# Attention kernel with a learned gate: how one right-hand operand of the gate product is formed in the setup

## The chip, the cores and the metric

The kernel runs on one core of a Trainium2 chip. The metric is device time in microseconds (us), the median of several executions. Lower is better. The core has five engines that run beside each other, each with its own queue of instructions worked off in order: TensorE (PE) multiplies matrices, VectorE (DVE), ScalarE (ACT) and GpSimd (POOL) work element by element, and SyncE (SP) issues DMAs. GpSimd issues DMAs as well, among them those that add what they bring to what is there.

## The reference

```python
memory_proj = einsum('bme,de->bmd', memory, W_mem)
scores = einsum('bnd,bmd->bnm', x, memory_proj) / sqrt(D)
attn = softmax(scores)
memory_context = einsum('bnm,bmd->bnd', attn, memory_proj)
gate = sigmoid(einsum('bnf,df->bnd', concat([x, memory_context]), W_gate) + b_gate)
fused = x + gate * memory_context
out = fused * rsqrt(mean(square(fused)) + EPS) * norm_w
```

Everything is float32. `x` is 8 x 1024 x 1024, the memory 8 x 64 x 512, `W_mem` 1024 x 512, `W_gate` 1024 x 2048.

## The kernel before

**The product with W1.** The gate needs `x` times the half of `W_gate` that meets `x`, here W1, 1024 x 1024. It is made for 512 rows of `x` at a time, 16 times (`q` = 0 to 15), by a scheme of Strassen's kind on two levels. The outer level cuts 512 x 1024 and W1 into quarters and needs seven *outer products* instead of eight, in the order 1, 6, 7, 5, 4, 2, 3 (`ORDER`). Each is split once more into seven *inner products* of TensorE, with the names `af`, `kB`, `kC`, `ed`, `ed`, `af`, `af` after the PSUM tiles that take them. The inner products need sums of quarters on both sides.

**Left sums** are made anew for every `q`. The outer ones (`s1` to `s4`, and one in place of the block `a21`) are made by VectorE (`outer_s`), from blocks of `x` that VectorE has transposed (`transpose_x`, L377). The inner ones (`l2`, four of 128x256 for each outer product) are made by GpSimd (`inner_s`). The `l2` tiles have two buffers. In the profile buffer numbers are left out, so `l2`, `t4` and `it4` are `l`, `t` and `it` there.

**Right sums** depend on W1 alone. They are made once, in the setup, and stay for all 16 blocks of rows. W1's quarters lie in two tiles `w1_0` and `w1_1`; `outer_b[2]`, the one this case is about, is the first half of `w1_1`. The outer operands 5, 7, 6 and 4 are formed from them one after another, where `W(h, c)` is a quarter in device memory:

- `t5` = quarter 7 - quarter 1, a VectorE subtraction of 128x2048 (`outer_sum`)
- quarter 7 in place: its negative by ScalarE (`outer_negative`, L216), then an adding DMA from GpSimd's queue brings `W(1, 1)` (`outer_add`, L220)
- `t6`: the negative of `t5`, then an adding DMA of `W(1, 1)`
- `t4`: the negative of `t6`, then an adding DMA of `W(1, 0)`

For every outer operand `inner_sum` makes four inner sums of 128x512: T1, T2, the quarter R12 in place, and T4. T1, T2 and T4 go to a tile `it`. `w1_place(o)` allocates the tiles. The sum of R12 overwrites a block of `t6`, so `t4`'s reading of `t6` has to come first.

**What sets the order.** The order is written by hand. All of these instructions are issued in program order on their engine (`pin`). The setup is a straight piece of code that ends with the memory side: `mg`, the projected memory times the other half of `W_gate`, is stored to `mgd` and read back by `load_mg`. The main loop counts slots, one for each inner product. `at(slot, ...)` puts an instruction behind a slot, and `mid` beside the work of an outer product. In the first 512 rows some right sums are still made in slots: those of operand 4 on GpSimd in slot 4, those of 2 and 3 on VectorE.

**What the rest of the first rows needs from those engines.** GpSimd adds parts of the products to the gate (`pre`, tile `gate`) and issues the DMA that adds the bias to `mg` (`add_bias`, L542). VectorE makes the sums `u` that free the PSUM banks of `kB` and `kC`, and adds `ed` and `af` to the gate. Before outer product 4 is over, `visit` adds the attention part on TensorE (tile `pc`), in the banks of its `kB` and `kC`.

Of the kernel before, what the change touches and what calls it, by code (L numbers as in the profile page):

```python
# [20 lines left out]
def tile_gated_cross_attention_rmsnorm(  # L21
# [42 lines left out]
    nc = tc.nc  # L64
# [30 lines left out]
    def tt(eng, o, a, b, op):  # L95
        pin(eng.tensor_tensor(o, a, b, op))  # L96
# [7 lines left out]
    def rows_by_chunk(w, n):  # L104

        return w.rearrange("(p j) f -> p j f", j=n)
# [57 lines left out]
    def w1_place(o):  # L164

        if o in (5, 6, 4):
            outer_b[o] = const.tile([P, 4, H], F32, tag=f"t{o}", name=f"t{o}")
        inner_t[o] = const.tile([P, 3, 2, C], F32, tag=f"it{o}", name=f"it{o}")

    def w_op(o, s):  # L170
        if s >= T4:
            return inner_t[o][:, s - T4, :, :]
        k, n = {R11: (0, 0), R21: (1, 0), R12: (0, 1), R22: (1, 1)}[s]
        return outer_b[o][:, 2 * k : 2 * k + 2, n * C : (n + 1) * C]
# [37 lines left out]
    def outer_sum(o, a, b):  # L212
        tt(nc.vector, outer_b[o], outer_b[a], outer_b[b], ALU.subtract)

    def outer_negative(o, b):
        pin(nc.scalar.activation(outer_b[o], outer_b[b], AF.Copy, scale=-1.0))  # L216

    def outer_add(o, h, c):
        rows = rows_by_chunk(w_gate_t[:D, :], KD)[:, 4 * h : 4 * h + 4, c * H : (c + 1) * H]
        pin(nc.gpsimd.dma_start(outer_b[o], rows, accum_op=ALU.add))  # L220

    def inner_sum(eng, o, n):
        s, a, b = ((T1, R12, R11), (T2, R22, T1), (R12, R22, R12), (T4, R21, T2))[n]
        tt(eng, w_op(o, s), w_op(o, a), w_op(o, b), ALU.subtract)
# [369 lines left out]
    def mg_product(l, r, pgs, start=False):  # L594
        for t in range(2):
            for k in range(KH):
                mm(pgs[t], l[:, k, t * P : (t + 1) * P], r[k], start and k == 0, k == KH - 1)
# [132 lines left out]
    for o, a, b in ((T1, w_op(7, R12), p11), (T2, p22, w_op(7, T1)), (R12, p22, w_op(7, R12)), (T4, p21, w_op(7, T2))):  # L730
        tt(nc.vector, w_op(7, o), a, b, ALU.subtract)
    w1_place(4)
    outer_negative(4, 6)
    for n in range(4):
        inner_sum(nc.gpsimd, 6, n)
    outer_add(4, 1, 0)
    mg_product(m22, b11, both)
    mg_copy(c21, both)
    store_mg(c21, 1, 0)
# [14 lines left out]
    def at(slot, fn, *args):  # L754
        due.setdefault(slot, []).append(lambda: fn(*args))
# [56 lines left out]

    for o in (2, 3):
        w1_place(o)
    for n in range(4):
        at(4, inner_sum, nc.gpsimd, 4, n)
    for s, o, n in ((3, 2, 0), (4, 2, 1), (5, 2, 2), (6, 2, 3), (11, 3, 0), (14, 3, 1), (14, 3, 3)):
        at(s, inner_sum, nc.vector, o, n)
# [416 lines left out]
```

## Time and profile before

| | us |
|---|---|
| median of 3 runs (950.52 to 951.43) | 951.36 |
| the profiled execution | 951.43 |
| its span, first to last instruction | 949.4 |
| busy in the span: DVE | 795.9 |
| busy in the span: ACT | 442.8 |
| busy in the span: POOL | 731.8 |

A row of a timeline reads: start, duration, engine, line, operation, `output<-inputs`, shape, count, and in brackets how long the engine stood idle before it and what ended that. Rows of one kind that follow each other are merged, so a duration can hold several instructions, and the durations of matmuls overlap a little. Nearly all helpers record their instructions in one line (`L93` for matmuls, `L96` for sums of two tensors), so the names of the tiles tell more than the line. In a table of stages each engine has its busy time and, in brackets, its count of instructions, in the order PE, PEld (weight load), DVE, ACT, POOL; the clock that TensorE was granted, the DMA share and GB/s follow.

### The profile page before, as it was taken

The page shows a single profiled execution, that of the slowest core. Times are in us where ns is not written, and L with a number is a line of the kernel's source. Part 1 is how long each engine was busy: PE and PEld are TensorE (multiplying, and loading weights), DVE is VectorE, ACT ScalarE, POOL GpSimd, SP SyncE. Part 2 cuts the span into 40 slices and gives each one's busy share as a digit, 9 for nine tenths or more (in the row PEclk, how much of TensorE's full clock was granted, in tenths as well). Part 3 has the DMA queues.
Part 4 walks back from the last instruction along what each step waited for, and adds up shares of the span by engine and source line. Part 5 has one row for each costly group of instructions (what it writes and reads, how often), then busy time and mean ns, then how long its engine had stood idle before and what let it go on. Part 6 is the DMA issues. An engine that isn't in the chain of part 4 may idle for free.

```text
span 949.4 us, 15989 instructions
## 1 busy us (share of the span) xinstructions
PE 934.1 (98%) x5584; PEld 733.4 (77%) x5584; DVE 795.9 (84%) x1275; ACT 442.8 (47%) x1125; POOL 731.8 (77%) x818
## 2 busy tenths in 40 slices
PE   9999899999999999999999999999999999999995
PEld 8746678787777878787777878787777878787774
DVE  6886688888898889888898889888897889888887
ACT  4343227364553627264553617264553617264556
POOL 4994978868696868868696868868696868868695
PEclk9999899999999999999999999999999999999998
DMA  9978197391927557391927456391927457391642
GB/s 376 309 157 189 23 155 156 75 204 45 203 87 151 117 124 154 78 201 45 208 81 156 111 127 151 79 204 41 209 81 156 112 126 153 81 205 40 133 154 89
DMA packets 72768, 131.59 MB, mean 139 GB/s; under 512 B 12656, under 2 KB 49520, under 8 KB 72432
## 3 DMA queue, kind: packets, MB, share of 16 engines
q1 hardware_dynamic: 61920, 93.86, 37.6%
q0 software_dynamic: 10768, 36.70, 21.3%
q8 instruction: 45, 0.74, 0.3%
q14 instruction: 35, 0.29, 0.1%
HBM read 90.70 MB, written 41.68 MB: 139 GB/s over the span
## 4 chain that ended last, share of the span: by engine, by line
PE 86%; POOL 6%; DVE 3%; DMA 3%; issue 1%; ACT 0%; POOLq 0%; DVEq 0%; ACTq 0%
PE af L93 30%; PE ed L93 20%; PE pc L93 10%; PE kC L93 10%; PE kB L93 10%; PE psT_af L93 5%; DMA t<-in_w_gate_t 3%; POOL it L96 1%; POOL gate L96 1%; POOL mg_right L96 1%; DVE gate L96 1%; POOL t_w L96 1%; POOL w L96 1%; POOL l L96 1%; DVE pm_it L96 0%
## 5 line engine op out<-in xcount | busy, mean ns | idle before, releaser
L96 POOL TENSOR_TENSOR gate<-gate,u 128x512 f32<-128x512 f32 (+1 forms) x224 | 244.9, 1107 | 152.1 <-DVE u L96 151.1
L833 ACT ACTIVATE gate<-gate 128x512 f32<-128x512 f32 x127 | 79.9, 630 | 183.4 <-DVE gate L96 182.1
L377 DVE STREAM_TRANSPOSE a<-xq 128x512 f32<-128x512 f32 x128 | 141.3, 1108 | 8.4 <-PE af L93 8.0
L96 POOL TENSOR_TENSOR l<-a 128x256 f32<-128x256 f32 x128 | 109.9, 859 | 15.9 <-PE af L93 15.9
L93 PE MATMUL kB<-it,l 128*128 128x256 f32 x448 | 116.1, 382 | 4.4 <-POOL l L96 4.4
L93 PE MATMUL pc<-mg,attnT 64*64 64x512 f32 x512 | 117.1, 596 | 0.1
L93 PE MATMUL ed<-it,l 128*128 128x256 f32 x448 | 115.1, 380 | 0.0
L862 DVE SCALAR_TENSOR_TENSOR gate<-gate,ss,nw_sb 128x512 f32<-128x512 f32 x120 | 110.4, 920 | 1.1
L1087 ACT COPY u<-af 128x256 f32<-128x256 f32 x112 | 41.4, 370 | 128.8 <-PE af L93 112.6
L93 PE MATMUL af<-w,a 128*128 128x256 f32 x384 | 98.6, 379 | 0.0
L93 PEld LDWEIGHTS kB<-it,l 128*128 128x128 f32 x448 | 85.7, 192 | 16.2 <-POOL l L96 4.8
L96 DVE TENSOR_TENSOR gate<-gate,ed 128x512 f32<-128x512 f32 x112 | 76.4, 682 | 25.0 <-POOL gate L96 23.1
L96 DVE TENSOR_TENSOR gate<-gate,pc 128x512 f32<-128x512 f32 x128 | 85.5, 677 | 11.8 <-ACT gate L833 11.8
L93 PEld LDWEIGHTS ed<-it,l 128*128 128x128 f32 x448 | 85.5, 191 | 11.4
L96 DVE TENSOR_TENSOR gate<-gate,af 128x512 f32<-128x512 f32 (+1 forms) x128 | 76.0, 604 | 13.3 <-PE af L93 10.5
L96 POOL TENSOR_TENSOR l<-s 128x256 f32<-128x256 f32 x96 | 83.5, 869 | 2.5 <-ACT u L1087 2.5
L93 PEld LDWEIGHTS af<-w,a 128*128 128x128 f32 x384 | 73.1, 190 | 10.2 <-issue 0.5
L93 PEld LDWEIGHTS pc<-mg,attnT 64*64 64x64 f32 x512 | 32.8, 132 | 49.7 <-issue 23.2
L93 PE MATMUL ed<-it,a 128*128 128x256 f32 x256 | 68.2, 390 | 0.0
L93 PE MATMUL af<-mg,attnT 64*64 64x512 f32 (+1 forms) x380 | 67.1, 457 | 0.0
L93 PE MATMUL kC<-w,l 128*128 128x256 f32 x256 | 66.6, 384 | 0.0
L96 DVE TENSOR_TENSOR u<-u,kB 128x256 f32<-128x256 f32 x112 | 45.8, 409 | 24.5 <-PE kB L93 23.7
(234 smaller groups left out, 2140.3 us busy)
## 6 DMA issues: line engine op xcount, KB each, us to landing
xq<-in_x SPq DMA_DIRECT2D x64, 512.0 KB, 10.4
gate<-in_x POOLq DMA_DIRECT2D x60, 512.0 KB, 8.5
out<-gate SPq DMA_DIRECT2D x60, 512.0 KB, 2.9
w<-in_w_gate_t SPq DMA_DIRECT2D x8, 512.0 KB, 10.2
w<-in_w_gate_t SPq DMA_DIRECT2D x2, 2048.0 KB, 16.9
mg<-mgd SPq DMA_DIRECT2D x16, 256.0 KB, 4.7
wm<-in_w_mem_t SPq DMA_DIRECT2D x4, 512.0 KB, 6.0
mpd<-mpT SPq DMA_DIRECT2D x4, 512.0 KB, 9.5
```

What stands on the lines that cost most here:

```text
L93: pin(nc.tensor.matmul(o, lhsT, rhs, start=start, stop=stop, skip_group_check=True))
L96: pin(eng.tensor_tensor(o, a, b, op))
L377: nc.vector.transpose(A[key][:, :, r * P : (r + 1) * P], chunks(xq[q][:, 4 * t : 4 * t + 4, :], KD)[:, half * KH : (half + 1) * KH],)
L833: pin(nc.scalar.activation(g, g, AF.Sigmoid))
L862: nc.vector.scalar_tensor_tensor(g[:, cols], g[:, cols], rstd[:, t % 2 : t % 2 + 1], nw_sb[:, cols], ALU.mult, ALU.mult,)
L1087: pin(nc.scalar.copy(p1, af[:, 0]))
```

## The change

`t4` is formed in one step on VectorE, quarter 2 less `t6`, where the negative on ScalarE and the adding DMA stood. Two of its four inner sums, T1 and T2, move from slot 4 of the main loop to the place in the setup where the adding DMA was issued. The other two stay in slot 4.

```diff
     w1_place(4)
-    outer_negative(4, 6)
+    outer_sum(4, 2, 6)
     for n in range(4):
         inner_sum(nc.gpsimd, 6, n)
-    outer_add(4, 1, 0)
+    for n in range(2):
+        inner_sum(nc.gpsimd, 4, n)
     mg_product(m22, b11, both)
...
-    for n in range(4):
+    for n in (2, 3):
         at(4, inner_sum, nc.gpsimd, 4, n)
```

On VectorE, at the end of the sums for operand 7 in the setup, the rows before were these (`it7` and `w1_0` belong to operand 7, `a22` is a transposed block of `x`, `s1` and `s2` are outer left sums, `u0` is a sum that frees a PSUM bank):

```order
L96 TENSOR_TENSOR w1_0_113<-pm_ed1_143,w1_0_113 128x2x256
L96 TENSOR_TENSOR it7_437<-w7_b_438,it7_437 128x512
L377 STREAM_TRANSPOSE a22_0_482<-xq0_306 128x4x128 x2
L96 TENSOR_TENSOR s1_0_490<-a21_0_429,a22_0_482 128x1024
L96 TENSOR_TENSOR s2_0_503<-s1_0_490,a11_0_426 128x1024
L96 TENSOR_TENSOR u0_1_512<-u0_1_512,kB0_1_519 128x256
```

Now, at the same place:

```order
L96 TENSOR_TENSOR w1_0_113<-pm_ed1_143,w1_0_113 128x2x256
L96 TENSOR_TENSOR it7_437<-w7_b_438,it7_437 128x512
L96 TENSOR_TENSOR t4_463<-w1_1_114,t6_399 128x2048
L377 STREAM_TRANSPOSE a22_0_483<-xq0_306 128x4x128 x2
L96 TENSOR_TENSOR s1_0_491<-a21_0_429,a22_0_483 128x1024
L96 TENSOR_TENSOR s2_0_504<-s1_0_491,a11_0_426 128x1024
L96 TENSOR_TENSOR u0_1_513<-u0_1_513,kB0_1_520 128x256
```

The sum for `t4` stands ahead of the last transposes of the first rows, so ahead of `s1` and `s2`, which need them. It reads `t6` and so waits for the adding DMA of `t6`.

On GpSimd, from the last sums of operand 6 to the left sums of outer product 7 (`l2_0_6` and `l2_0_7` are left sums of the products 6 and 7), the difference is:

```order
 L96 TENSOR_TENSOR t6_399<-t6_399 128x2x256
 L96 TENSOR_TENSOR it6_400<-t6_399,it6_400 128x512
-L220 DMA t4_463<-in_w_gate_t 128x4x512
-L96 TENSOR_TENSOR l2_0_6_516<-s2_0_503 128x256
-L96 TENSOR_TENSOR l2_0_6_516<-l2_0_6_516,s2_0_503 128x256
-L96 TENSOR_TENSOR l2_0_6_516<-s2_0_503 128x256
-L96 TENSOR_TENSOR l2_0_6_516<-s2_0_503,l2_0_6_516 128x256
 L96 TENSOR_TENSOR it4_464<-t4_463 128x512
 L96 TENSOR_TENSOR it4_464<-t4_463,it4_464 128x512
+L96 TENSOR_TENSOR l2_0_6_517<-s2_0_504 128x256
+L96 TENSOR_TENSOR l2_0_6_517<-l2_0_6_517,s2_0_504 128x256
+L96 TENSOR_TENSOR l2_0_6_517<-s2_0_504 128x256
```

The DMA is gone, and two of the `it4` sums stand ahead of the left sums of product 6 instead of behind them. The other two, and the left sums of product 7, follow as before. On ScalarE only the negative of `t6` is gone.

## The prediction

> **What bounds the kernel now.** I read the page's head first, then who TensorE (PE) waits for, then PE's timeline round the wait, and last the timelines of the three engines that feed it.
>
> ```profile
> span 949.4 us, 15989 instructions
> ...
> PE 934.1 (98%) x5584; PEld 733.4 (77%) x5584; DVE 795.9 (84%) x1275; ACT 442.8 (47%) x1125; POOL 731.8 (77%) x818
> ...
> PE kB L93 <- POOL l L96: 4.4, 1, 4.4
> PE pz L93 <- DVE zeros L116: 1.2, 1, 1.2
> ```
>
> PE is the bound: busy 98% of the span. Setup work matters only where PE waits for it, and in the view of PE's waits only two are listed. One is the start. The other is a single wait of 4.4 us, of a `kB` product for an `l` sum of GpSimd (POOL).
>
> ```profile
> 87.74 1.13 PE L93 MATMUL af<-t,s 128*128 128x256 f32 x4
> ...
> 93.89 1.03 PE L93 MATMUL af<-w,a 128*128 128x256 f32 x4
> 99.28 2.08 PE L93 MATMUL kB<-it,l 128*128 128x256 f32 x4 [4.36 <-POOL l L96]
> 101.14 1.92 PE L93 MATMUL kC<-w,l 128*128 128x256 f32 x4
> 102.85 1.79 PE L93 MATMUL ed<-it,a 128*128 128x256 f32 x4
> ...
> 107.07 1.03 PE L93 MATMUL af<-t,s 128*128 128x256 f32 x4
> ...
> 123.10 1.03 PE L93 MATMUL af<-w,a 128*128 128x256 f32 x4
> ...
> 129.15 1.03 PE L93 MATMUL af<-w,s 128*128 128x256 f32 x4
> ```
>
> PE's timeline shows the place. Outer product 7 of the first 512 rows begins at 93.89, outer product 5 at 107.07: 13.18 us. Undisturbed, seven inner products take 129.15 - 123.10 = 6.05 us, 0.86 each. So **product 7 loses 13.18 - 6.05 = 7.13 us**: 4.36 of waiting, and 2.77 more because the rows behind the wait are 1.8 to 2.1 us long instead of 1.03. The stages say why; the column behind POOL is the granted PE clock:
>
> ```profile
> 98.00:100.00 2.00, 0.72 (x2) 0.64 (x3) 0.00 (x0) 0.00 (x0) 1.92 (x4) 0.50 0.00 0
> 102.00:104.00 2.00, 2.00 (x6) 1.65 (x5) 1.97 (x4) 0.37 (x1) 1.92 (x3) 0.50 0.00 0
> 106.00:108.00 2.00, 2.00 (x11) 1.77 (x10) 1.90 (x4) 1.63 (x8) 1.52 (x2) 1.00 0.00 0
> ```
>
> The clock is 0.50 behind the wait and 1.00 again by 106. Why GpSimd was late is in its own timeline:
>
> ```profile
> 69.79 1.29 POOL L96 TENSOR_TENSOR it<-t 128x512 f32<-128x512 f32 x1 [1.28 <-DMA t<-in_w_gate_t]
> ...
> 73.62 2.25 POOL L96 TENSOR_TENSOR it<-t,it 128x512 f32<-128x512 f32 x1
> 75.82 1.29 POOL L220 DMA_DIRECT2D t<-in_w_gate_t  x1
> ...
> 81.72 1.17 POOL L96 TENSOR_TENSOR l<-s,l 128x256 f32<-128x256 f32 x1
> 92.70 1.27 POOL L96 TENSOR_TENSOR it<-t 128x512 f32<-128x512 f32 x1 [9.80 <-DMA t<-in_w_gate_t]
> ...
> 97.70 0.72 POOL L96 TENSOR_TENSOR l<-a 128x256 f32<-128x256 f32 x1
> 98.50 0.72 POOL L96 TENSOR_TENSOR l<-l,a 128x256 f32<-128x256 f32 x1
> ...
> 100.54 1.94 POOL L96 TENSOR_TENSOR gate<-gate,u 128x512 f32<-128x512 f32 x2
> ...
> 129.00 1.27 POOL L96 TENSOR_TENSOR gate<-gate,u 128x512 f32<-128x512 f32 x1 [1.48 <-DVE u L96]
> ```
>
> The adding DMA for `t4` is issued at 75.82, and GpSimd then stands 9.80 us for its landing, with the four sums of `it4` and the four of `l` for product 7 queued behind. PE's `kB` needs the second `l` sum, which ends at 99.22; it starts at 99.28.
>
> **The change part by part.** *Removed: the wait for the DMA.* `t4` becomes a VectorE (DVE) sum, so GpSimd never stands for a landing at 92.70. What is late next is either one of GpSimd's own earlier jobs or an input of `l`. I follow both, against these DVE rows:
>
> ```profile
> 70.23 0.68 DVE L96 TENSOR_TENSOR it<-w_b,it 128x512 f32<-128x512 f32 x1
> 71.32 2.13 DVE L377 STREAM_TRANSPOSE a<-xq 128x512 f32<-128x512 f32 x2 [0.41 <-PE pm_ctx L93]
> 73.49 1.26 DVE L96 TENSOR_TENSOR s<-a,a 128x1024 f32<-128x1024 f32 x1
> 78.19 1.23 DVE L96 TENSOR_TENSOR s<-s,a 128x1024 f32<-128x1024 f32 x1 [3.44 <-PE pm_ed L93]
> ...
> 88.59 1.22 DVE L96 TENSOR_TENSOR a<-a,a 128x1024 f32<-128x1024 f32 x1
> ...
> 101.84 0.69 DVE L96 TENSOR_TENSOR gate<-gate,ed 128x512 f32<-128x512 f32 x1 [9.06 <-POOL gate L96]
> ```
>
> *Added: one DVE sum of 128x2048, behind the row at 70.23.* The setup has one of the same shape (`t5`), beside two GpSimd subtractions:
>
> ```profile
> 27.15 3.14 DVE L96 TENSOR_TENSOR t<-w 128x2048 f32<-128x2048 f32 x1 [0.58 <-DMA w<-in_w_gate_t]
> ...
> 26.88 1.28 POOL mg_right L96
> 28.22 3.20 POOL mg_right L96
> ```
>
> DVE's 3.14 us include waiting: GpSimd's first subtraction ends at 28.16, DVE at 30.29, so the sum itself is about 2.13, and GpSimd's second takes 3.20 instead of 1.28. The two take turns. Bounds 2.13 to 3.14. I take 2.13 from the end of GpSimd's running subtraction (69.79 + 1.29 = 71.08), so `t4` is ready at **73.2** (at most 74.1).
>
> *What is queued behind it on DVE:* two transposes (2.13), the sum `s1` (1.26) and `s2` (1.23). They end at 75.3 and about 76.9. The sum `s2` can't begin before 78.15, when PE lets its buffer go: 3.44 us of idle time hide the added sum, at worst with a port turn of about 1.3 too many.
>
> *SyncE's (SP's) queue:* the next `x` load waits for the transposes, so it goes 2 to 3 us later (75.3 to 76.5). Its first transpose stands beyond 108 now; the landing takes at most 17.8 us in the view of that tile (estimate: by 94.3). Hidden. The stores and the load of `mg` behind it are the third rival.
>
> *GpSimd:* the second sum of `it6` waits out the DVE sum (to 74.5), and its third waits for it by dependence: DVE reads the block that this sum overwrites. They end at 75.7 and, with a DVE turn of 1.1, at 78.1. Then the two new `it4` sums, 2 x 1.27 and a turn of 1.2 for `s2`: 81.8. Now the `l` sums of product 6, first at 79.56 before, begin 2.3 us later. Four take 2.9 (97.70 to 100.54), so the second ends at 83.3, at most 84.5 with a small DVE turn each. PE's `kB` of product 6 starts at 87.74 + 0.97 = 88.71. Hidden, with 4 us in hand. The last two `it4` sums then end between 87.2 and 89.4.
>
> *Moved: the `l` sums of product 7.* Their operand is the `a<-a,a` sum of DVE, ready at 88.59 + 1.22 = 89.8 (91.1 if a GpSimd sum of 1.27 gets ahead of it). So GpSimd is there in time, or nearly, and DVE's sum sets the start. The second `l` ends 1.52 us later (97.70 to 99.22), at **91.3 to 92.6**. PE wants it at 93.89 + 2 x 0.43 = 94.75. The wait goes, with 2.1 to 3.4 us in hand, and with it the slow clock: 7.13 us on PE.
>
> *Removed as well:* ScalarE's (ACT's) negative (1.9 us) and GpSimd's issue (1.29). Neither was on a path that PE felt; I count nothing.
>
> *What is late next.* From 92.70 on GpSimd has no idle time of a microsecond until 129.00, and DVE stands 9.06 us for its `gate` sum. They run just ahead of PE:
>
> ```profile
> 115.49 0.40 DVE L96 TENSOR_TENSOR u<-u,kB 128x256 f32<-128x256 f32 x1
> ...
> 115.94 0.65 PE L93 MATMUL pc<-mg,attnT 64*64 64x512 f32 x2
> ```
>
> Ten inner products after 107.07 PE could start `pc` at 107.07 + 6.05 + 3 x 0.86 = 115.70; it starts at 115.94, behind DVE's `u` at 115.89. So `pc` sits at the meeting of two chains. PE's moves by 7.13, or 7.37 if those 0.24 go too. The GpSimd and DVE chain moves by as much as the `gate` sum of 100.54: it now begins when the four `l` sums end, 2.9 us after 89.8 to 91.1, and up to 0.6 later for the one DVE sum that falls among them: 92.7 to 94.6, or **7.8 to 5.9 us earlier**. Most of that span lies beyond or at PE's 7.13. I take 7.0.
>
> Sum: 951.43 (the profiled execution: span 949.4 and 2.0 around it) - 7.0 = **944.4 us**. It is 0.07 above the median of 951.36, which changes nothing.
>
> Two rules of the Trainium skill, weighed. SBUF — State Buffer (Who interferes with whom) says that VectorE and GpSimd share one port pair under an exclusive lock, held for a whole instruction. That speaks against a 2.13 us sum put into GpSimd's busiest stretch. The row of 3.20 agrees. With every turn charged by that rule (2.13 and 1.07 twice, 0.55 four times), GpSimd comes to the `l` sums at an estimated 89.4, and without it at 84: both before 89.8, so the sum is the same.
>
> TensorE: Matmul & The Clock Gate (What's actually happening) says that an idle window of about 3.4 us halves the clock, and a busy one restores it. At half rate for one such window the loss here would be 4.36 + 1.7 = 6.1 us, an estimate, and the time 945.4. The rows show 2.77 for the slow part, and I use these.
>
> **The rivals.**
>
> *1. The feeding chain decides.* If port turns fall badly, `gate` begins at 94.6 or a little later, and `pc` waits up to 2 us for DVE. Gain 5 to 6.5: 945 to 946.5 us. For it: DVE and GpSimd are both full there, and `pc` follows DVE within 0.05 us already. Against: `l` waits for one early DVE sum, not for GpSimd.
>
> *2. The wait moves to `t6` and the kernel gets slower.* DVE now stands in order for the adding DMA of `t6`, which only ACT and GpSimd did.
>
> ```profile
> 69.80 1.92 ACT L216 ACTIVATE t<-t 128x2048 f32<-128x2048 f32 x1 [7.46 <-DMA t<-in_w_gate_t]
> ...
> DMA to landing us min/median/max: 8.9/11.4/16.8
> ```
>
> Issued at 58.27, it landed at 69.7, 1.2 us before DVE gets there. If it lands d later, GpSimd comes to the `l` sums of product 7 not at 87.2 to 89.4 but d later. From d = 3.8 to 6.0 on (arrival after 94.75 - 1.52 = 93.2) `kB` waits again, and from d = 8.3 to 10.5 on (arrival after 97.70, as now) the kernel is slower than before, by each further us. With a landing at 82 (d = 12.3) that is 1.8 to 4.0 us: 953.2 to 955.4. For it: the same kind of DMA took 16.8 when the `x` load ran beside it (d = 5.4: `gate` begins 2.2 to 5.0 earlier than now, 946.4 to 949.2 us). Against: what runs before 69.7 is unchanged, and the `x` load is still issued behind it.
>
> *3. The gain is handed to `mg`.* GpSimd's bias DMA waits for the second `mg` load, which waits for a store.
>
> ```profile
> SPq L99 <- DMA mgd<-mg_c: 14.5, 1, 14.5
> ...
> 108.82 0.85 POOL L542 DMA_DIRECT2D mg<-in_b_gate  x1
> ```
>
> That load was issued at 94.3 and landed 3.4 us later or more, about 98. The bias DMA will be wanted at 101.8. All 3 us of delay on SP's queue would still fit to within a microsecond, and the 1 MB of `t4` that ran beside it is gone. If the load came at 108 instead, nothing would be gained: 951.4 us.
>
> That the change doesn't do what it says I exclude: the order of instructions shows the DMA gone.
>
> **How the numbers follow.** Forecast, full or nearly full return of the 7.13 (943.8 to 944.9): 0.68. First rival, or `t6` a little late (945 to 949): 0.20. Gain lost, third rival: 0.05. Slower, second: 0.03. More than forecast (below 943.5, a wait not visible here): 0.04. The low end is 951.43 - 7.37 less 0.5, since the runs shown differ by 0.9; the high end takes in most of the first rival. Two in ten are left out. About 0.2%, 1.9 us, is what a measurement of this kernel can tell from no change; so faster is 0.68 + 0.20 + 0.04 = 0.92, same 0.05, slower 0.03.
>
> **What would show it.** `t4` on DVE at 71 to 73.2, 2.1 to 3.1 us long. No wait over 1 us on GpSimd between 70 and 79. The `l` sums of product 7 near 90, released by DVE. No `kB` in PE's waits, a granted clock of 1.00 from 88 to 116. Product 5 at 99.9 to 100.0, `pc` at 108.6 to 109.5. A `pc` that waits for DVE would show the first rival, a DVE sum that starts late with the `t6` DMA as releaser the second, GpSimd standing before the bias DMA the third. I am wrong if PE waits anywhere between 75 and 116, or if time lost later in the first 512 rows eats what is won.

## The result, and the profile after

| | before | after |
|---|---|---|
| median, us (6 runs each) | 950.70 | 944.37 (944.11 to 945.00) |
| ratio of the two | | 0.9932, 95% interval 0.9919 to 0.9945 |
| the profiled execution, us | 951.43 | 944.16 |
| its span, us | 949.4 | 942.3 |

The changed kernel is faster by 0.68% (0.55 to 0.81), between 5 and 8 us. The profiled executions differ by 7.3, their spans by 7.1; the medians differ by 6.3, mainly because the profiled execution of the kernel before was the longest of its six. The views below are those read of the kernel before, now of the changed kernel.

First the page's head and the view of who PE waits for:

```profile
span 942.3 us, 15986 instructions
...
PE 931.5 (99%) x5584; PEld 730.3 (77%) x5584; DVE 801.3 (85%) x1276; ACT 441.3 (47%) x1124; POOL 733.6 (78%) x817
...
PE pz L93 <- DVE zeros L116: 1.2, 1, 1.2
```

Only the wait at the start is left. The wait of `kB` for `l` is gone. Next, PE's timeline round the place, and then the view by stages (columns as before: the clock stands behind POOL):

```profile
94.04 1.03 PE L93 MATMUL af<-w,a 128*128 128x256 f32 x4
94.90 1.03 PE L93 MATMUL kB<-it,l 128*128 128x256 f32 x4
...
100.08 1.03 PE L93 MATMUL af<-t,s 128*128 128x256 f32 x4
...
108.85 0.65 PE L93 MATMUL pc<-mg,attnT 64*64 64x512 f32 x2
```

```profile
96.00:98.00 2.00, 2.00 (x11) 1.77 (x10) 1.97 (x4) 0.62 (x3) 1.92 (x3) 1.00 0.00 0
...
100.00:102.00 2.00, 2.00 (x11) 1.77 (x10) 1.17 (x3) 0.51 (x3) 2.00 (x2) 1.00 0.00 0
```

Product 7 of the first 512 rows takes 100.08 - 94.04 = 6.04 us, where it took 13.18. The rows are 1.03 us long throughout and the granted clock is 1.00. The attention product `pc` starts at 108.85 instead of 115.94: 7.09 us earlier, and the span is 7.1 shorter. So all of the gain lies ahead of `pc`.

The timelines of VectorE (DVE) and GpSimd (POOL) in the changed stretch:

```profile
70.99 3.30 DVE L96 TENSOR_TENSOR t<-w,t 128x2048 f32<-128x2048 f32 x1
74.22 2.10 DVE L377 STREAM_TRANSPOSE a<-xq 128x512 f32<-128x512 f32 x2
76.35 1.60 DVE L96 TENSOR_TENSOR s<-a,a 128x1024 f32<-128x1024 f32 x1
78.34 1.82 DVE L96 TENSOR_TENSOR s<-s,a 128x1024 f32<-128x1024 f32 x1 [0.39 <-PE pm_ed L93]
...
88.74 1.22 DVE L96 TENSOR_TENSOR a<-a,a 128x1024 f32<-128x1024 f32 x1
```

```profile
69.53 1.27 POOL L96 TENSOR_TENSOR it<-t 128x512 f32<-128x512 f32 x1 [0.95 <-DMA t<-in_w_gate_t]
70.88 1.27 POOL L96 TENSOR_TENSOR it<-t,it 128x512 f32<-128x512 f32 x1
74.37 1.27 POOL L96 TENSOR_TENSOR t<-t 128x512 f32<-128x512 f32 x1 [2.23 <-DVE t L96]
...
76.83 2.26 POOL L96 TENSOR_TENSOR it<-t 128x512 f32<-128x512 f32 x1
79.16 2.13 POOL L96 TENSOR_TENSOR it<-t,it 128x512 f32<-128x512 f32 x1
81.26 0.73 POOL L96 TENSOR_TENSOR l<-s 128x256 f32<-128x256 f32 x1
...
86.59 1.72 POOL L96 TENSOR_TENSOR it<-t,it 128x512 f32<-128x512 f32 x1
90.10 0.72 POOL L96 TENSOR_TENSOR l<-a 128x256 f32<-128x256 f32 x1 [1.79 <-DVE a L96]
...
93.41 1.95 POOL L96 TENSOR_TENSOR gate<-gate,u 128x512 f32<-128x512 f32 x2
```

The added VectorE sum runs from 70.99 to 74.29. It costs GpSimd 2.23 us of waiting and takes VectorE's idle time before `s<-s,a` from 3.44 to 0.39; that sum still starts when PE lets it, at 78.34 instead of 78.19. GpSimd is done with the right sums of operand 4 at 88.31 and then stands 1.79 us for the operand of the `l` sums of product 7. They begin at 90.10, not 97.70, and the `gate` sums behind them at 93.41, not 100.54: 7.13 us earlier.

### The profile page after: what moved, and what is told of

Its sections match the earlier page's. It is cut to its first block, busy times and chain, and to the rows that moved or that the text cites. A ratio compares the mean times of both kernels' runs of the same rounds, so it can differ in the third digit from the quotient of the medians.

```text
span 942.3 us, 15986 instructions
## 1 busy us (share of the span) xinstructions
PE 931.5 (99%) x5584; PEld 730.3 (77%) x5584; DVE 801.3 (85%) x1276; ACT 441.3 (47%) x1124; POOL 733.6 (78%) x817
## 4 chain that ended last, share of the span: by engine, by line
PE 96%; DVE 1%; POOL 1%; ACT 0%; issue 0%; POOLq 0%; ACTq 0%
PE af L93 32%; PE ed L93 21%; PE kC L93 10%; PE kB L93 10%; PE pc L93 10%; PE psT_af L93 5%; PE pm_ctx L93 2%; PE pm_af L93 2%; PE pm_ed L93 2%; DVE gate L96 1%; POOL gate L96 1%; PE mg_u L93 1%; PE psT_ed L93 0%; PE pz L93 0%; PE psT_b L93 0%; POOL l L96 0%
## 5 line engine op out<-in xcount | busy, mean ns | idle before, releaser
L93 PE MATMUL af<-t,s 128*128 128x256 f32 x256 | 65.8, 379 | 0.0
```

What stands on the lines that cost most here:

```text
L93: pin(nc.tensor.matmul(o, lhsT, rhs, start=start, stop=stop, skip_group_check=True))
```

## The experiments

Before the runs two chains met in `pc`. One is PE's own: its wait and its slow clock. The other is GpSimd's and VectorE's: `l` sums of product 7, `gate`, and the VectorE and ScalarE work behind it up to the sums `u` that free the banks for `pc`. Both had moved by 7.1, so the two profiles did not settle which one decides. The runs bear on that, and take the change apart. Each ratio below is to runs of the kernel before that were taken on the same occasion.

### VectorE's sum alone

In the changed kernel, all four inner sums of operand 4 are made in slot 4 again:

```diff
-    for n in range(2):
-        inner_sum(nc.gpsimd, 4, n)
...
-    for n in (2, 3):
+    for n in range(4):
         at(4, inner_sum, nc.gpsimd, 4, n)
```

> VectorE's sum for t4 alone; all four it4 sums stay in slot 4. Theory W (the gain is GpSimd's lost wait for the adding DMA): GpSimd makes the l sums of product 6 from 79.6, then four it4 sums of 1.27 plus turns, and reaches the l sums of product 7 at 88 to 91, about when their operand is ready (89.96 in the changed kernel). No kB wait, 944.4 to 945.2 us. Rival M (moving two sums ahead is needed as well): GpSimd comes 2 us or more too late, pc waits for it, 946.4 or more.

Measured: 944.92 us (944.37 to 945.60), ratio to before 0.9938 (0.9926 to 0.9951). No `kB` wait. GpSimd in this run:

```profile
79.51 0.72 POOL L96 TENSOR_TENSOR l<-s 128x256 f32<-128x256 f32 x1 [3.08 <-ACT u L1086]
...
87.86 1.27 POOL L96 TENSOR_TENSOR it<-t,it 128x512 f32<-128x512 f32 x1
90.36 0.73 POOL L96 TENSOR_TENSOR l<-a 128x256 f32<-128x256 f32 x1 [1.23 <-DVE a L96]
```

All four sums fit between 82.8 and 89.1, and GpSimd still waits 1.23 us for VectorE. Replacing the DMA brings the gain. The move of the two sums is worth 0.2 us in the spans and 0.55 in the medians, which these runs do not separate from nothing.

### The DMA kept, the sums behind it put off

In the kernel before:

```diff
     for n in range(4):
-        at(4, inner_sum, nc.gpsimd, 4, n)
+        at(17, inner_sum, nc.gpsimd, 4, n)
```

> The kernel before, DMA and negative kept, but the four it4 sums in slot 17, behind the l sums of products 7 and 5. Theory W (nothing but the wait at kB counts): the wait is gone, 944.4 us. Theory F (what counts is that the sums fill GpSimd's idle time of 83 to 90): GpSimd still idles there, the 5.1 us of sums land in its full stretch after 99, pc or product 4 waits up to 5 us, 948 to 949.5 us, with no wait at product 7 and the clock at 1.00 there.

Measured: 949.53 us (949.17 to 949.90), ratio 0.9987 (0.9978 to 0.9996). The `l` sums of product 7 now start as early as in the changed kernel, after GpSimd has idled 7.04 us, and product 7 runs undisturbed. But the four sums then stand in the full stretch:

```profile
90.00 0.73 POOL L96 TENSOR_TENSOR l<-a 128x256 f32<-128x256 f32 x1 [7.04 <-DVE a L96]
...
93.32 1.95 POOL L96 TENSOR_TENSOR gate<-gate,u 128x512 f32<-128x512 f32 x2
...
101.63 1.27 POOL L96 TENSOR_TENSOR it<-t 128x512 f32<-128x512 f32 x1
```

PE in the same run:

```profile
108.73 1.13 PE L93 MATMUL af<-t,a 128*128 128x256 f32 x4 [2.54 <-DVE gate L96]
```

PE waits 2.54 us in product 4 and `pc` starts at 113.07. Theory F holds (its range ended at 949.5): to end the wait of `kB` is not enough. The change gains because `t4` is ready before GpSimd's idle time, so that the 5 us of sums fill it.

### All four sums early

In the changed kernel:

```diff
-    for n in range(2):
+    for n in range(4):
         inner_sum(nc.gpsimd, 4, n)
...
-    for n in (2, 3):
-        at(4, inner_sum, nc.gpsimd, 4, n)
```

> All four it4 sums in the setup behind those of operand 6. The l sums of product 6 begin 2.5 to 3.5 us later than at 81.26 of the changed kernel, the second ends by 86.6; PE wants it at 88.86. Theory W with slack: hidden, 944.4 us within 0.5. Rival (the l sums of product 6 are already tight): a kB wait in product 6 and 945.5 us or more.

Measured: 944.07 us (944.02 to 944.47), ratio 0.9929 (0.9917 to 0.9941). No `kB` wait; the second `l` sum of product 6 ends at 86.05, 2.8 us before PE wants it, and those of product 7 start at 90.05. This is the lowest median of all, but the interval of its ratio overlaps that of the changed kernel: no difference is shown.

### The sum on GpSimd

In the changed kernel:

```diff
-    outer_sum(4, 2, 6)
+    tt(nc.gpsimd, outer_b[4], outer_b[2], outer_b[6], ALU.subtract)
```

> The sum for t4 on GpSimd instead of VectorE (128x2048, about 5 us from four of 1.27); everything else as in the changed kernel. Theory W: GpSimd loses 5 us but no longer waits 2.23 for VectorE nor 1.1 for its port; it reaches the l sums of product 7 at 89.8 to 90.5 instead of 90.10: 944.4 to 945.0 us. Rival (VectorE is what brings it): GpSimd 3 us or more late, 946.5 us or more.

Measured: 945.80 us (945.25 to 946.88), ratio 0.9948 (0.9935 to 0.9962).

```profile
69.36 4.55 POOL L96 TENSOR_TENSOR t<-w,t 128x2048 f32<-128x2048 f32 x1 [0.79 <-DMA t<-in_w_gate_t]
...
91.32 0.73 POOL L96 TENSOR_TENSOR l<-a 128x256 f32<-128x256 f32 x1
```

The expectation missed: GpSimd comes at 91.32, without idle time, about 0.9 us later than its operand would allow, so the time falls between the two theories. VectorE seems the better place, by 1.1 us in the spans and 1.4 in the medians; the times of the two kernels do not overlap, but they were taken on different occasions and the intervals of the two ratios do. Most of the gain comes on either engine.

### How much lateness costs: the last sum made three, six and nine times

In the changed kernel, with `k` = 2, 5 and 8. The extra sums write the same values again.

```diff
     for n in (2, 3):
         at(4, inner_sum, nc.gpsimd, 4, n)
+    for _ in range(k):
+        at(4, inner_sum, nc.gpsimd, 4, 3)
```

> The changed kernel with the last it4 sum made three times instead of once: GpSimd 2.5 to 3.6 us more in slot 4. It stood 1.79 us idle there, so the l sums of product 7 begin 0.8 to 2.0 us later. Theory C (the chain l, gate, VectorE, pc binds): pc waits that much longer, 945.2 to 946.4 us, no kB wait. Rival K (PE's own kB decides, which has 3.3 us in hand): 944.4 us.

> The last it4 sum made six times: GpSimd 6.4 to 8 us more, l sums of product 7 begin 4.6 to 6.3 us later, kB waits 1.3 to 3.0 us. Theory C: pc follows the chain, 949.0 to 950.7 us. Rival K: only the kB wait counts, 945.7 to 947.4 us. The clock: if a wait this short leaves it at 1.00, the slow clock needs a longer wait; if it falls to 0.50 in any case, K gives 2.8 us more.

> The last it4 sum made nine times: GpSimd 10.2 to 12.5 us more, kB waits 5 to 7.5 us and the clock falls to 0.50 as before the change. Theory C: 952.8 to 955.1 us. Rival K: wait plus 2.8 us of slow clock, 952.2 to 954.7 us; here the two can't be told apart, and the run is for the clock against the shorter wait of the run with six.

Measured: 945.70 us (945.54 to 946.09) with three, ratio 0.9946 (0.9931 to 0.9961); 949.76 (949.30 to 950.64) with six, 0.9991 (0.9981 to 1.0000); 953.91 (953.51 to 954.67) with nine, 1.0036 (1.0024 to 1.0047). Here are PE's waits with three of the sums, the start left out, and then the longest of its waits with six:

```profile
PE af L93 <- POOL l L96: 1.1, 1, 1.1
PE pc L93 <- DVE u L96: 0.2, 1, 0.2
```

```profile
PE kB L93 <- POOL l L96: 2.6, 1, 2.6
```

With three there is no `kB` wait at all, and the kernel is still 1.3 us slower than the changed one (2.0 in the spans): rival K is out. The `af` wait named with `l` is of another kind. The `l` sums of product 5 had ended at 101.06, 5 us before that `af` started at 106.06. It also waits for ScalarE's copy out of `af`, which ended at 105.92:

```profile
104.82 0.83 ACT L518 COPY attnT<-attnT 64x256 f32<-64x256 f32 x2 [2.35 <-DVE attnT L512]
105.56 0.36 ACT L1090 COPY u<-af 128x256 f32<-128x256 f32 x1
```

That copy stands behind the copies of `attnT`, which wait for VectorE, which stood for the late `gate` sum: the same chain, felt by PE at one more place.

With six the clock fell, so K with 2.8 us of slow clock gives 948.5 to 950.2, and the median does not tell the two theories apart. The ten executions do, as far as their mean granted clocks show it. Five have 0.995, like the profiled one, in which the clock fell; four have 0.997, like the profiled execution of the changed kernel, in which it did not. The medians of the two groups are 949.75 and 949.79 us: a clock that stayed up won nothing. (Only the profiled one has a trace.) With nine, both theories give the measured time.

### t6 late

In the changed kernel:

```diff
-    outer_add(6, 1, 1)
     for n in range(4):
         inner_sum(nc.gpsimd, 5, n)
+    outer_add(6, 1, 1)
```

> The changed kernel with t6's adding DMA issued behind the four it5 sums, 5.1 us later (a test of the rival in which the wait moves to t6, d about 5). VectorE stands for the landing with its transposes behind it. Theory R: the sum for t4 starts at 74.5 to 76.5, GpSimd comes to the l sums of product 7 at 92 to 93.5 instead of 90.1, pc 2 to 3.4 us later, 946.4 to 947.8 us, no kB wait. Rival (GpSimd's and VectorE's idle times take all of it): 944.4 us.

Measured: 947.69 us (947.30 to 947.81), ratio 0.9966 (0.9953 to 0.9979). GpSimd waits 5.59 us for the landing, which comes 4.8 us later than in the changed kernel, and reaches the `l` sums at 93.81, 0.3 later than the range allowed. PE then waits in a few places, 1.3 us at most, and not for the `kB` of product 7. So this rival's price was right: the landing 4.8 us later takes 3.3 us of the gain back.

### What all of them have in common

For each profiled execution, the start of the `gate` sums behind the `l` sums of product 7, the start of the first `pc`, and the span (us):

| run | `gate` | `pc` | between | span | span less `pc` |
|---|---|---|---|---|---|
| all four early | 93.36 | 108.77 | 15.41 | 942.2 | 833.4 |
| after | 93.41 | 108.85 | 15.44 | 942.3 | 833.5 |
| VectorE's sum alone | 93.67 | 109.09 | 15.42 | 942.5 | 833.4 |
| sum on GpSimd | 94.52 | 109.93 | 15.41 | 943.4 | 833.5 |
| last sum three times | 95.37 | 110.78 | 15.41 | 944.3 | 833.5 |
| t6 late | 97.00 | 112.40 | 15.40 | 945.9 | 833.5 |
| last sum six times | 99.93 | 115.33 | 15.40 | 948.8 | 833.5 |
| before | 100.54 | 115.94 | 15.40 | 949.4 | 833.5 |
| last sum nine times | 102.81 | 118.22 | 15.41 | 951.7 | 833.5 |
| DMA kept, sums put off | 93.32 | 113.07 | 19.75 | 947.5 | 834.4 |

From `gate` to `pc` it is 15.40 to 15.44 us in nine kernels, with a `kB` wait in product 7 of nothing, 2.6, 4.4 or 6.7 us and with the slow clock or without it. What follows `pc` is the same to 0.1 us. The exception fits: its four sums were put into this very stretch. These are the links in the changed kernel:

```profile
94.72 0.69 DVE L96 TENSOR_TENSOR gate<-gate,ed 128x512 f32<-128x512 f32 x1 [1.59 <-POOL gate L96]
...
99.58 2.18 POOL L96 TENSOR_TENSOR gate<-gate,u 128x512 f32<-128x512 f32 x1 [0.47 <-DVE u L96]
101.79 0.69 DVE L96 TENSOR_TENSOR gate<-gate,ed 128x512 f32<-128x512 f32 x1 [0.83 <-POOL gate L96]
...
108.36 0.44 DVE L96 TENSOR_TENSOR u<-u,kB 128x256 f32<-128x256 f32 x1
```

Between them VectorE works without a break, and none of them waits for PE; `pc` starts 0.05 us after the last one. So theory C holds: **the chain behind the `l` sums sets the time, and PE's own wait, with its slow clock, ran beside it.**

How narrowly it does so is part of the finding. From the start of product 5, PE alone needs 6.05 + 3 x 0.86 = 8.63 us to `pc`. By that it could have started `pc` 0.24 us sooner than it did before the change, 0.14 sooner in the changed kernel, and between 0.1 and 4.5 sooner in the other runs. So both chains had to become shorter. They did so together, because the same `l` sums feed both. No run shortens the feeding chain and keeps PE's wait; by these numbers it would have won no more than the 0.24.

## Why the prediction was right, point by point

- *The time.* Forecast 944.4, measured 944.37; 7.0 us were to go in the profiled execution, and 7.1 of the span went. That the median agrees to 0.03 us is luck: the sum starts from 951.43, the longest of six executions of the kernel before, whose median came out at 950.70, and between medians the gain is 6.3. The executions of the kernel before lie between 948.9 and 951.9 us over all occasions.
- *The wait for the DMA, and what is late next.* As forecast, the operand from VectorE sets the start of the `l` sums (released by `DVE a`), the second one ends at 91.63 (forecast 91.3 to 92.6), and `gate` begins at 93.41 (92.7 to 94.6).
- *The 7.13 us on PE, split into 4.36 of waiting and 2.77 of slow clock.* The size was right, the role only in part. The prediction saw two chains of about one length meet at `pc`, gave PE's loss as the gain, and let the sum rest on both. The runs show that the feeding chain is the later one each time. With the last sum made six times PE loses 105.64 - 94.99 - 6.05 = 4.6 us to wait and slow clock, and `pc` still waits 0.15 us for VectorE. In the changed kernel PE alone could have started `pc` at 100.08 + 8.63 = 108.71, only 0.14 us sooner than it did. The two chains are so nearly equal there that both reckonings gave one number.
- *The first rival* was this chain, given as a loss against the forecast. Its mechanism was the true one; its price was not paid because `gate` came at 93.41, not at 94.6.
- *The added sum.* Forecast to end at 73.2, at most 74.1; it ended at 74.29. The step that failed: VectorE was to get its turn when GpSimd's first sum ended, but GpSimd's second went first (70.88 to 72.15). The landing came 0.26 us earlier than before, so GpSimd's first sum was over at 70.80, and its second began 0.11 us ahead of VectorE's. So the row of `t4` was 3.30 us long (2.1 to 3.1 were given). The mark "no wait over 1 us on GpSimd between 70 and 79" was therefore wrong, with 2.23 us. The idle time before 90.10 hid it: 1.79 us were left.
- *Small misses.* Product 5 starts at 100.08 (99.9 to 100.0 were given), because product 7 already starts 0.15 us later. The end of `s1`, given as about 76.9, adds up to 76.6 from the terms beside it; it came at 77.95, as both sums took longer. Neither bears on the total.
- *The `l` sums of product 6:* 81.26, forecast 81.8. Hidden, and still hidden when they start 2.8 us later (all four early).
- *The second rival, `t6`.* Made late in a run of its own, it cost 3.3 us for a delay of 4.8, within the 2 to 5 us given for about 5. In the changed kernel the DMA landed in time.
- *The third, `mg`.* The bias DMA was issued at 101.70 (forecast 101.8) without a wait. SyncE waited 10.1 us for the store instead of 14.5.

## What to carry to other kernels

Where two engines' chains meet at one instruction, the wait that the profile lists on the bounding engine need not be the price: measure the distance from the feeding chain's last free step to the meeting point, and see whether it stays the same when the wait changes. When the two chains are about equally long, only what shortens both is gain. A DMA that makes an operand out of data already on the chip can cost little itself and yet keep the next engine's work out of its idle time. What counts is then where the queued work lands, as the run with the sums put off shows: no wait at the old place, and four fifths of the gain gone.

## What the runs showed of the hardware that was not expected

The granted clock fell after a wait of 2.65 us (last sum six times), but not after one of 2.54 (DMA kept, sums put off). The stages behind the wait with six sums:

```profile
99.00:100.00 1.00, 1.00 (x5) 0.85 (x4) 0.00 (x0) 0.27 (x2) 1.00 (x3) 0.72 0.00 0
100.00:102.00 2.00, 2.00 (x7) 1.53 (x6) 0.77 (x2) 0.09 (x1) 2.00 (x3) 0.50 0.00 0
102.00:103.00 1.00, 1.00 (x4) 0.81 (x3) 1.00 (x2) 0.28 (x1) 0.92 (x2) 0.57 0.00 0
```

And those round the wait with the sums put off:

```profile
106.00:108.00 2.00, 0.19 (x1) 0.00 (x0) 0.00 (x0) 0.00 (x0) 2.00 (x4) 1.00 0.00 0
108.00:110.00 2.00, 1.13 (x4) 0.68 (x4) 1.74 (x4) 0.02 (x1) 1.92 (x4) 1.00 0.79 131
```

In the first run the clock drops within a microsecond of PE's resuming at 98.67, and 1.95 us are lost to it (4.60 less 2.65). If it is 0.50 or 1.00 at any moment, these means put the slow stretch at 99.44 to 102.86, an estimate of 3.42 us. The same reckoning from stages of 1 us gives 97.56 to 104.40 in the kernel before and 99.88 to 106.72 with nine sums: 6.84 us each, twice as much. The Trainium skill, TensorE: Matmul & The Clock Gate (What's actually happening), gives an idle window of about 3.4 us, free-running. Slow stretches of once and twice 3.42 us agree with that length, and two waits of nearly one length with different outcomes fit a free-running window. If the window is that long, PE was not idle for all of it when the wait was 2.65 us; how much is enough these cases do not settle.

Which engine goes first when VectorE's two-input sum and a GpSimd sum come together changed from run to run. In these traces the one whose row starts first goes first, and a tenth or two of a microsecond decides. In the changed kernel GpSimd's second `it6` sum starts 0.11 us ahead of VectorE's sum and goes first (1.27 us long, then 2.23 us of waiting for VectorE). It starts 0.16 to 0.38 us ahead in four more runs, and goes first in each. With the last sum made nine times VectorE's sum starts 0.16 us ahead (70.75), and GpSimd's stands beside it:

```profile
70.91 3.27 POOL L96 TENSOR_TENSOR it<-t,it 128x512 f32<-128x512 f32 x1
```
